# A second layer's set-up and edge scores placed in the wait for the first layer's expert rows, in a four-layer graph network on one core

## The chip, the cores and the metric

The kernel runs on one core of one Trainium2 chip. Its time is the device time of one execution in microseconds (us); the metric is the median over several executions. The core has five engines that run their own instruction streams side by side: TensorE (PE, matrix products), VectorE (DVE), ScalarE (ACT), GpSimd (POOL, which here issues the indirect gathers and scatters) and SyncE (SP, which here issues most of the plain DMAs). Each stream is in order: an instruction that waits holds back everything behind it on its engine.

## The reference, cut to what matters

The program takes `x` [3125, 256], 50,000 edges sorted by their target, and 32 attributes per edge. It runs four layers one after the other, and each layer is a graph part, a dense mixing part and a feed-forward part of experts, all added to `x`. What matters here is the feed-forward part of the first layer (L0), in which each token goes to one of 8 experts, and the graph part of the second layer (L1), a graph attention with 4 heads of 64:

```
# L0 feed-forward (top 1, capacity 489 tokens an expert)
x = x + prob * (relu(xe @ w1[e] + b1[e]) @ w2[e] + b2[e])     # xe: rows of layernorm(x)

# L1 graph part
x_proj = (xn @ lin_W.T).reshape(n, 4, 64)
s_src = einsum(x_proj, att_src); s_dst = einsum(x_proj, att_dst)
att = leaky(s_src[src] + s_dst[dst] + einsum((ea @ lin_edge_W.T), att_edge))
alpha = exp(att - segment_max(att, dst)); alpha = alpha / (sum over dst + 1e-12)
out = segment_sum(x_proj[src] * alpha, dst) + bias
```

The term with `ea` depends on the edges' attributes and on weights alone, not on `x`.

## The kernel before, in words

Tokens lie in 25 tiles of 128 rows, edges in 391 columns of 128. All of it is Python that writes one program; a scheduler then orders the instructions of each engine by the order in which they were written and by its own estimate of when each could start. Many lines are helpers: L145 is a matrix product, L153 and L155 are the copies out of PE's banks on ACT and DVE, L201 and L221 the layer norm, L425 and L419 the indirect scatter and gather.

**The first layer's experts.** `l0_ffn` (L1378) does the routing on DVE (softmax, first maximum, running counts: L331 to L1423), writes the 3,125 normed rows into the table `moe_buf` with 25 indirect scatters on POOL, and then goes through 8 experts. Of each it loads `w1`, `w2` (1 MB each) and `b2`, and the expert's rows `xb` (four loads, L1440); PE transposes them (L1445, into `xT`), multiplies by `w1` into `hT` and by `w2` into `y`. The `xb` loads wait for all 25 scatters. After the last expert, a check (`fin_ok`, L1474) decides a branch; in the branch taken, 25 gathers `yt` on POOL fetch the experts' rows, which are added to `x`, and the layer norm is worked out again.

**Work sent along.** Beside the experts run two other things. `route_scans` works out tables for a later layer on DVE and ACT. `Pump` issues the `cells` sends, 391 indirect scatters on POOL that fill a table of layer L2: 16 ahead of the experts, then one for every 700 columns that PE multiplies in `l0_ffn`, each bound to a product so that it doesn't run ahead, then 32 after the second layer's graph part, and the rest paced by products in `l1_ffn`, the second layer's experts. The pump is stopped after the last expert's products are written.

**The second layer's graph part.** After the branch, in this order of the program: `breaks` (L955) makes the masks `pen` and `penc`, which say where one target's edges end, out of 20 `dh` loads and one `dhc` load. `l1_near_setup` (L1551) loads weights, among them 12 small pieces of the attention vectors into `bd`, fills the table `l1seed` with a large negative number, makes 8 more columns of the weight `linw` and the 16-column weight `vedge`, and works out `sidx`, the place of each target's first edge. Then it goes through the 25 tiles (L1595 to L1604): a product `row` with the new columns, copies, a DMA that writes the row into the table `l1rows`, and a scatter of four numbers into `l1seed` (the seeds, L425, on POOL). It adds the bias to `x` (L1606), and `spread` (L983) reads the seeds back as `sh` and carries them to all edges by four scans into `pre`.

Then `drive` weaves four generators together. `gat_near` fetches the 391 columns of source rows with indirect gathers (L1072) into a `ring` of 44 places, adds `pre` to them (`att`), finds the maxima over each target, scales the rows, and sums them with PE (`seg`, L499); a ring place is free once its `seg` has run. `l1_mix_lean` is the dense mixing part, `norm_after` the norm that follows, and `l1_edge_scores` (L1610) works out the edges' own scores in 25 rounds: load 256 KB of `ea`, a product of 16 rows by 512 columns (L1619), a copy by ACT to `ez` (L1621), four small transposes (L1624), and an addition on DVE to `pre` (L1626). It has one `ez` buffer and two `ea` buffers.

Of the kernel before, what the change touches and what calls it, by code (L numbers as in the profile page):

```python
# [18 lines left out]
P = 128  # L19
# [100 lines left out]
class Net:  # L120
# [861 lines left out]

    def spread(self, pool, pre, seed, penc):  # L983

        nc = self.nc
        w = P + HALO
        per = penc.shape[0]
        sh = pool.tile([per, 4, w, 4], F32, name="sh")
        self.after_all(seed.name, nc.sync.dma_start(sh, self.lin(seed, 0, [[P * 4, per], [per * P * 4, 4], [1, w * 4]])))
        ps = [self.ps(4 * per) for _ in range(4)]  # L990
        for h in range(4):
            se = pool.tile([per, 4, w], F32, name="se")
            nc.vector.tensor_tensor_scan(se.rearrange("p q i -> p (q i)"), penc.rearrange("p q i -> p (q i)"),
                                         sh.rearrange("p q i h -> p (q i) h")[:, :, h], 0.0, OP.add, OP.max)
            for q in range(4):
                nc.tensor.transpose(ps[q][:, h * per:(h + 1) * per], se[:, q, HALO:], self.ident[:per, :per])
        for q in range(4):
            v = pre[:, q * per:(q + 1) * per, :]
            self.evac(v, ps[q].rearrange("p (h c) -> p c h", h=4))

# [376 lines left out]

    def l0_ffn(self, pool, lean=False, pr=None):  # L1378
        nc, a = self.nc, self.a
# [50 lines left out]
        mt = [(i * P, min(P, CAP - i * P)) for i in range(4)]  # L1430
        for e in range(NE):
            w1 = pool.tile([P, 2, FF], F32, name="w1", bufs=2)
# [3 lines left out]
            b2 = pool.tile([P, D], F32, name="b2", bufs=2)  # L1436
            nc.sync.dma_start(b2, bcast_rows(a["L0_ffn_b2"][e], D))
            xb = pool.tile([P, 4, D], F32, name="xb", bufs=2)
            for i, (m0, m) in enumerate(mt):
# [46 lines left out]
    def l0_combine(self, pool, ybuf, ri, prob):  # L1486

        nc = self.nc
        big = pool.tile([P, 2, D], F32, name="big")
        nc.vector.memset(big[:, 0, :], 1.0e4)  # L1490
        nc.vector.memset(big[:, 1, :], -1.0e4)
        top = 3.4028234663852886e38
        for t in range(T):
            y = self.gather(pool, "yt", ybuf, ri[:, t:t + 1], D, 4)
            nc.vector.tensor_scalar(y, y, prob[:, t:t + 1], None, op0=OP.mult)
            o = pool.tile([P, D], F32, name="yo", bufs=2)
            m = pool.tile([P, D], I32, name="ym", bufs=3)
            nc.vector.memset(o, 0.0)
            nc.vector.tensor_tensor(m, y, y, op=OP.is_equal)
            nc.vector.copy_predicated(o, m, y)  # L1500
            for j, (op, lim) in enumerate(((OP.is_gt, top), (OP.is_lt, -top))):
                m = pool.tile([P, D], I32, name="ym", bufs=3)
                nc.vector.tensor_scalar(m, o, lim, None, op0=op)
                nc.vector.copy_predicated(o, m, big[:, j, :])
            nc.vector.tensor_add(self.x[:, t, :], self.x[:, t, :], o)
# [44 lines left out]

    def l1_near_setup(self, keep, pool, pre, penc):  # L1551


# [13 lines left out]
        for k in range(2):  # L1567
            p = self.ps(8)
            self.mm(p, [(wn[:, o, k * P:(k + 1) * P], bd[:, o, :8]) for o in range(2)])
            nc.vector.tensor_copy(w[:, k, D:], p)  # L1570
        vb = keep.tile([P, 16], F32, name="vedge")
        nc.vector.memset(vb, 0.0)
# [8 lines left out]
        sidx = pool.tile([P, T], I32, name="sidx")  # L1581
        self.first_edges(sidx, self.deg)
        nrow = 393 * P
        seed = self.dram.tile([nrow, 4], F32, name="l1seed")
        neg = pool.tile([P, 262], F32, name="neg")
        nc.vector.memset(neg, -BIG)
        nc.sync.dma_start(self.lin(seed, 0, [[nrow * 4 // P, P], [262, 6], [1, 262]]),
                          neg[:, None, :].to_broadcast([P, 6, 262]))
# [3 lines left out]
        row = [pool.tile([P, 4, 66], F32, name=f"row{i}") for i in range(3)]  # L1592
        for r in row:
            nc.vector.memset(r[:, :, 64:65], 1.0)
        for t in range(T):  # L1595
# [14 lines left out]
    def l1_edge_scores(self, pool, pre, vb):  # L1610

        nc, a = self.nc, self.a
        pv = pre.rearrange("p (q j) h -> p j q h", q=4)
        for j0 in range(0, EG, 4):
            m = min(4, EG - j0)
            ea = pool.tile([P, 4 * P], F32, name="ea", bufs=2)
            nc.sync.dma_start(ea[:, :m * P], a["eaT"][:, j0 * P:(j0 + m) * P])
            p = self.ps(m * P, parts=16)
            nc.tensor.matmul(p, vb, ea[:, :m * P], start=True, stop=True)  # L1619
            ez = pool.tile([16, 4 * P], F32, name="ez")  # L1620
            nc.scalar.copy(ez[:, :m * P], p)  # L1621
            p = self.ps(16 * m)
            for j in range(m):
                nc.tensor.transpose(p[:, j * 16:(j + 1) * 16], ez[:, j * P:(j + 1) * P], self.ident[:16, :16])  # L1624
            v = pv[:, j0:j0 + m]
            nc.vector.tensor_add(v, v, p.rearrange("p (j q h) -> p j q h", q=4, h=4))  # L1626
            yield

# [925 lines left out]
    def route_scans(self, pool):  # L2554
# [3 lines left out]
        nc = self.nc  # L2558
        S, n = 4, C2
        lo = pool.tile([P, T2, n], BF16, name="r_lo")  # L2560
# [11 lines left out]
        for t in range(0, T2, S):  # L2572
            d = pool.tile([P, S, n], F32, name="r_d")
            wi = pool.tile([P, S, n], I32, name="r_wi")
            wl = pool.tile([P, S, n], I32, name="r_wl")
            out = pool.tile([P, 2, S, n], BF16, name="r_out")
# [504 lines left out]
    def fast(self):  # L3081
# [3 lines left out]
        with tc.tile_pool(name="keepf", bufs=1) as keep, tc.tile_pool(name="dramf", bufs=1, space=DRAM) as dram:  # L3085
# [30 lines left out]
            self.px = None  # L3116
            with Banks(self, **plain):
                send = self.send(cells, place, value[:, :, None], C1)
                for _ in range(16):
                    next(send)  # L3120
                with tp("ffn0") as p, tp("scan4") as sp:
                    self.pump = Pump(tc, send, 700)
                    beside(self.l0_ffn(p, True, pr0), (self.route_scans(sp), 1, 3))


            with tp("att1") as gp:
# [3 lines left out]
                nc.vector.tensor_scalar(nodeg, self.deg, 0.5, -BIG, op0=OP.is_lt, op1=OP.mult)  # L3130
                pen, penc = self.breaks(gp, self.dlin, C1)
                part, add_part = self.part_sums(keep)
                with Banks(self, **plain), tp("set1") as p:
                    table, aself, vb = self.l1_near_setup(gp, p, pre, penc)
# [5 lines left out]
                with Banks(self, mm=2, acc=1, ga=2, seg=2, px=1), tp("mix1") as mp:  # L3140
                    self.numbers()
                    self.one_hots = 2
                    close = self.gat_close(gp, table, 64, aself, nodeg, 1e-12, add_x)
                    drive((self.gat_near(gp, g, table, pre, pen, 64, close, RING, 12), 4), (self.l1_mix_lean(mp), 1),
                          (self.norm_after(closed, self.mixed, then=add_part), 1), (self.l1_edge_scores(mp, pre, vb), 2))
            self.px = None
# [365 lines left out]
```

## Time and profile before

The median of four executions is 3753.76 us (3748.79 to 3765.47). The profiled execution took 3758.31 us, with a span of 3756.2 us, so 2.1 us lie around the span. All times below are of the profiled execution.

| | us |
|---|---|
| PE busy in the span | 2946.5 (78%) |
| POOL busy | 2356.1 (63%) |
| DVE busy | 1885.0 (50%) |
| ACT busy | 890.6 (24%) |
| routing done (`wi`), first `moe_buf` scatter | 744.51, 744.98 |
| first `xb` load issued, first transpose of it | 778.48, 780.57 |
| last product of the last expert; `fin_ok`; first `yt` gather | 1017.81, 1020.00, 1031.86 |
| DVE goes on after the branch | 1077.42 |
| first seed scatter, first ring gather | 1114.48, 1146.95 |
| first `ea` load of the edge scores, first product | 1168.02, 1174.30 |

Busy time is the time in which an engine executes, summed over the span; the table's moments are us from the start of the span. Two instructions on different engines overlap, so busy times don't add up to the span. The granted clock (PEclk) is the share of full speed that TensorE was allowed.

### The profile page before, as it was taken

How to read it: one execution, taken by the hardware profiler on the slowest of the kernel's cores; microseconds unless marked ns; L12 is line 12 of the kernel's file. 1: busy time of each engine (PE TensorE's matmuls, PEld its weight loads, DVE VectorE, ACT ScalarE, POOL GpSimd, SP SyncE). 2: the span in 40 equal slices, each digit the busy share in tenths (PEclk: the TensorE clock that was granted, in tenths of full speed). 3: DMA queues.
4: the chain of work that ended last, by engine and by line, in shares of the span. 5: the costliest groups of instructions: out<-in, count | busy, mean ns of one | idle time of the engine just before them, and what ended most of it. 6: DMA issues, size and time to landing. Idle time of an engine off the chain costs nothing. (4 is left out here: it accounts for less than half of the span.)

```text
span 3756.2 us, 41484 instructions
## 1 busy us (share of the span) xinstructions
PE 2946.5 (78%) x12101; PEld 2093.4 (56%) x12101; DVE 1885.0 (50%) x5664; ACT 890.6 (24%) x1851; POOL 2356.1 (63%) x2316
## 2 busy tenths in 40 slices
PE   7576788569845766665998999369679899679999
PEld 3244565346532544543676888248556577457666
DVE  3176574431174966765991323531484711535665
ACT  2101001122111211111333211323222233334544
POOL 0368767667737777776775677467757664037771
PEclk9787787679956877877998999679889999789999
DMA  4897884433134434432224445158565523401110
GB/s 150 281 316 244 270 295 111 129 123 122 44 95 141 115 108 112 114 102 77 52 52 136 128 138 158 41 181 258 173 209 151 165 69 106 122 13 22 18 17 15
DMA packets 398304, 485.52 MB, mean 129 GB/s; under 512 B 100756, under 2 KB 317280, under 8 KB 397809
## 3 DMA queue, kind: packets, MB, share of 16 engines
q1 hardware_dynamic: 214128, 257.09, 22.8%
q0 software_dynamic: 88160, 129.89, 12.5%
q10 hardware_dynamic: 95776, 95.77, 7.6%
q8 instruction: 99, 1.62, 0.2%
q14 instruction: 141, 1.15, 0.1%
HBM read 324.71 MB, written 157.76 MB: 128 GB/s over the span
## 5 line engine op out<-in xcount | busy, mean ns | idle before, releaser
L540 POOL DMA_INDIRECT G<-h_tab,gi x391 | 415.8, 1064 | 282.3 <-DMA cl_w<-in_weight 119.9
L425 POOL DMA_INDIRECT cells<-count,turned x391 | 398.0, 1018 | 174.2 <-PE seg L905 60.3
L425 POOL DMA_INDIRECT cells<-value,place x391 | 421.0, 1077 | 132.9 <-PE mm L145 65.5
L905 PE MATMUL seg<-H,cells 128*128 128x256 f32 (+1 forms) x1875 | 478.9, 400 | 18.7 <-DMA cells<-cells 12.3
L1072 POOL DMA_INDIRECT ring<-l1rows,e1src x391 | 407.7, 1043 | 125.6 <-issue 74.0
L905 PEld LDWEIGHTS seg<-H,cells 128*128 128x128 f32 x1875 | 352.6, 191 | 101.4 <-DMA cells<-cells 20.9
L145 PE MATMUL mm<-w,hT 128*128 128x256 f32 (+1 forms) x1712 | 405.0, 388 | 0.0
L145 PE MATMUL mm<-xnT,w 128*128 128x512 f32 (+1 forms) x896 | 382.1, 568 | 6.4 <-DVE x L2876 5.9
L499 PE MATMUL seg<-G,E 128*128 128x257 f32 x782 | 270.5, 478 | 128.5 <-DMA G<-h_tab,gi 91.8
L425 POOL DMA_INDIRECT by_dst<-rec4i,place4i x256 | 263.2, 1028 | 161.7 <-issue 48.2
L145 PEld LDWEIGHTS mm<-w,hT 128*128 128x128 f32 (+1 forms) x1712 | 312.4, 190 | 55.7 <-issue 15.5
L499 PE MATMUL seg<-ring,E 128*128 128x264 f32 x782 | 255.9, 487 | 73.0 <-DVE E L493 72.7
L1072 POOL DMA_INDIRECT ring<-l3rows,e2src x256 | 243.7, 952 | 98.5 <-PE mm L145 32.6
L499 PEld LDWEIGHTS seg<-G,E 128*128 128x128 f32 x782 | 164.8, 231 | 219.7 <-DMA G<-h_tab,gi 108.9
L499 PEld LDWEIGHTS seg<-ring,E 128*128 128x128 f32 x782 | 181.3, 242 | 128.5 <-DVE E L493 84.2
L145 PEld LDWEIGHTS mm<-xnT,w 128*128 128x128 f32 x896 | 155.0, 194 | 133.3 <-issue 117.3
L201 PE MATMUL mm<-ident,xn 128*128 128x128 f32 x400 | 82.3, 360 | 161.0 <-DVE xn L221 116.9
L201 PEld LDWEIGHTS mm<-ident,xn 128*128 128x128 f32 x400 | 61.3, 183 | 181.9 <-DVE xn L221 70.0
L493 DVE TENSOR_TENSOR E<-px,e1dl 128x512 f32<-128x512 f32 x196 | 133.6, 682 | 31.9 <-PE seg L499 26.7
L1087 DVE TENSOR_TENSOR ring<-ring,px 128x1040 f32<-128x1040 f32 x98 | 120.3, 1227 | 1.1 <-ACT px L1063 1.0
L145 PE MATMUL mm<-xT,w 128*128 128x489 f32 x256 | 111.3, 593 | 7.3 <-DVE xT L155 7.3
L505 ACT COPY W_side<-seg 64x257 f32<-64x257 f32 (+2 forms) x126 | 40.9, 325 | 280.6 <-PE seg L499 272.1
(774 smaller groups left out, 5229.6 us busy)
## 6 DMA issues: line engine op xcount, KB each, us to landing
cells<-zeros ACTq DMA_DIRECT2D x80, 1024.0 KB
cells<-cells SPq DMA_DIRECT2D x250, 320.0 KB
ws<-in_L_ffn_expert_w SPq DMA_DIRECT2D x90, 256.0 KB
w<-in_L_ffn_w SPq DMA_DIRECT2D x16, 1024.0 KB
h_tab<-htab_s SPq DMA_DIRECT2D x25, 512.0 KB
r_b<-rowa SPq DMA_DIRECT2D x64, 128.0 KB
xb<-x_exp SPq DMA_DIRECT2D x30, 256.0 KB
y_exp<-ys ACTq DMA_DIRECT2D x30, 256.0 KB
```

Source lines behind the costliest of these rows:

```text
L145: m = self.nc.tensor.matmul(out, l, r, start=(i == 0), stop=(i == last))
L201: self.nc.tensor.transpose(p[:, i * P:(i + 1) * P], src(t0 + i)[:, k * P:(k + 1) * P], self.ident)
L425: return self.nc.gpsimd.indirect_dma_start(out=table, out_offset=bass.IndirectOffsetOnAxis(ap=idx, axis=0), in_=src, in_offset=None, bound ...
L493: nc.vector.tensor_tensor(A["hot"][:, :m], self.io(P)[:, None, :].to_broadcast([P, m, P]), g["dl"][:, c:c + m, None].to_broadcast([P, m, P ...
L499: self.product = nc.tensor.matmul(A["sum"], e, rows_c, start=(c == 0 or window(c - 1, nt) != k), stop=last).ins
L505: nc.scalar.copy(out, a[:, :w])
L540: nc.gpsimd.indirect_dma_start(out=ring[i % len(ring)][:, :wide], out_offset=None, in_=table, in_offset=bass.IndirectOffsetOnAxis(ap=gidx[ ...
L905: self.product = nc.tensor.matmul(acc, b[:, d * P:(d + 1) * P], h[:, i, :], start=(i == 0), stop=(i == T - 1)).ins
L1072: got = nc.gpsimd.indirect_dma_start(out=ring[:, i % size].rearrange("p h f -> p (h f)"), out_offset=None, in_=table, in_offset=bass.Indir ...
L1087: nc.vector.tensor_mul(v, v, EX[c // CB][:, c % CB:c % CB + m, :, None] .to_broadcast([P, m, 4, d + 1]))
```

## The change

1. `l1_near_setup` becomes a generator in three parts. The first runs ahead of `l0_ffn`: its loads, the `l1seed` fill and `sidx`. The second is handed to `l0_ffn` as `fill`, and is called after the 25 scatters and the first expert's weight loads are written: `vedge`, the 8 columns of `linw`, and all 25 rounds of `l1_edge_scores`. The third runs after the experts and writes table rows and seeds.
2. The edge scores use the room of the tile `hT` (four places for `ea`, three for `ez`); the transposes lag two rounds behind; the result is copied to `pre` and not added. They are no longer woven into `gat_near`. `spread` now adds to `pre`.
3. The masks (`breaks`) are made after the rows and ahead of `spread`.
4. In `l0_ffn`, the weights of the next expert are loaded ahead of the rows of this one, and the pump is stopped ahead of the last expert's products with `w2` (8,192 columns).
5. To make room, the branch that isn't taken (`l0_combine`) uses `hT`'s room too, and `route_scans` works on 2 columns at a time where it was 4, twice as often.

```diff
@@ spread
-            v = pre[:, q * per:(q + 1) * per, :]
-            self.evac(v, ps[q].rearrange("p (h c) -> p c h", h=4))
+            v, s = pre[:, q * per:(q + 1) * per, :], ps[q].rearrange("p (h c) -> p c h", h=4)
+            if add:
+                nc.vector.tensor_add(v, v, s)
+            else:
+                self.evac(v, s)
@@ l0_ffn
-        for e in range(NE):
+        W = {}
+
+        def weights(e):
             w1 = pool.tile([P, 2, FF], F32, name="w1", bufs=2)
...
+        weights(0)
+        if fill is not None:
+            fill(pool.tile([P, FF // P, CAP], F32, name="hT").rearrange("p f c -> p (f c)"))
+        for e in range(NE):
+            if e + 1 < NE:
+                weights(e + 1)
+            w1, w2, b2 = W.pop(e)
             xb = pool.tile([P, 4, D], F32, name="xb", bufs=2)
...
+            if e == NE - 1:
+                self.pump = None
             for i, (m0, m) in enumerate(mt):
@@ l1_near_setup (loads, seed table, neg, row, sidx now ahead of this)
+        room = yield
+        vb = pool.tile([P, 16], F32, name="vedge")
...
+        self.l1_edge_scores(room, pre, vb)
+        yield
         table = self.dram.tile([NP, D + 8], F32, name="l1rows")
...
-        self.spread(pool, pre, seed, penc)
-        return table, aself, vb
+        yield table, aself
+        with self.tc.tile_pool(name="sprd", bufs=1) as tmp:
+            self.spread(tmp, pre, seed, masks.pop(), add=True)
+        yield
@@ l1_edge_scores
+        def turn(j0, m, ez):
+            p = self.ps(16 * m)
+            for j in range(m):
+                nc.tensor.transpose(p[:, j * 16:(j + 1) * 16], ez[:, j * P:(j + 1) * P], self.ident[:16, :16])
+            nc.vector.tensor_copy(pv[:, j0:j0 + m], p.rearrange("p (j q h) -> p j q h", q=4, h=4))
+        for i, j0 in enumerate(range(0, EG, 4)):
+            m = min(4, EG - j0)
+            o = i % 4 * 512
+            ea = room[:, o:o + m * P]
+            nc.sync.dma_start(ea, a["eaT"][:, j0 * P:(j0 + m) * P])
+            p = self.ps(m * P, parts=16)
+            nc.tensor.matmul(p, vb, ea, start=True, stop=True)
+            o = 2048 + i % 3 * 512
+            ez = room[:16, o:o + m * P]
+            nc.scalar.copy(ez, p)
+            behind.append((j0, m, ez))
+            if len(behind) > 2:
+                turn(*behind.pop(0))
@@ the program
+                setup = self.l1_near_setup(gp, set1.__enter__(), pre, masks)
+                with Banks(self, **plain):
+                    next(setup)
...
+                        beside(self.l0_ffn(p, True, pr0, setup.send), (self.route_scans(sp), 2, 3))
+                    table, aself = next(setup)
+                set1.__exit__(None, None, None)
+                mask = tp("mask1")
+                pen, penc = self.breaks(mask.__enter__(), self.dlin, C1)
+                masks.append(penc)
+                with Banks(self, **plain):
+                    next(setup)
...
                     drive((self.gat_near(rp, g, table, pre, pen, 64, close, RING, 12), 4), (self.l1_mix_lean(mp), 1),
-                          (self.norm_after(closed, self.mixed, then=add_part), 1), (self.l1_edge_scores(mp, pre, vb), 2))
+                          (self.norm_after(closed, self.mixed, then=add_part), 1))
```

In the scheduled program of after, SP's stream holds the set-up's loads and the `l1seed` fill, the first expert's weights, 14 of the 25 `ea` loads (the second expert's weights among them), the first `xb` load, and then the other 11 `ea` loads between the `xb` loads of the first two experts. On PE all 25 rounds of the edge scores stand ahead of the first `xb` transposes. On DVE the `bd`, `neg` and `row` fills, the sums of `sidx` and four copies of `line` stand ahead of the routing's first softmax step. After the branch, two reductions of the mixing part (L1645) and the bias stand ahead of the first table row, and ten or so further operations of the mixing part lie between the rows; on SP 8 of the 20 `dh` loads stand ahead of the rows' DMAs, and the other mask loads and `sh` behind them.

More of the change, by code (lines that the diff above doesn't have):

```diff
@@ L981, in breaks, with spread @@
         return pen, penc
-    def spread(self, pool, pre, seed, penc):
+    def spread(self, pool, pre, seed, penc, add=False):
         nc = self.nc
@@ L1376, in l0_gate, with l0_ffn @@
         return pr, gate
-    def l0_ffn(self, pool, lean=False, pr=None):
+    def l0_ffn(self, pool, lean=False, pr=None, fill=None):
         nc, a = self.nc, self.a
@@ L1437, in l0_ffn @@
             nc.sync.dma_start(b2, bcast_rows(a["L0_ffn_b2"][e], D))
+            W[e] = w1, w2, b2
+        weights(0)
[5 more added lines that the diff above has]
+            w1, w2, b2 = W.pop(e)
             xb = pool.tile([P, 4, D], F32, name="xb", bufs=2)
@@ L1488, in l0_combine @@
         nc = self.nc
-        big = pool.tile([P, 2, D], F32, name="big")
-        nc.vector.memset(big[:, 0, :], 1.0e4)
-        nc.vector.memset(big[:, 1, :], -1.0e4)
+        room = pool.tile([P, 8, CAP], F32, name="hT").rearrange("p f c -> p (f c)")
+        part = lambda i: room[:, i * D:(i + 1) * D]
+        nc.vector.memset(part(0), 1.0e4)
+        nc.vector.memset(part(1), -1.0e4)
         top = 3.4028234663852886e38
@@ L1495, in l0_combine @@
             nc.vector.tensor_scalar(y, y, prob[:, t:t + 1], None, op0=OP.mult)
-            o = pool.tile([P, D], F32, name="yo", bufs=2)
-            m = pool.tile([P, D], I32, name="ym", bufs=3)
+            o = part(2 + t % 2)
+            m = part(4).bitcast(I32)
             nc.vector.memset(o, 0.0)
@@ L1501, in l0_combine @@
             for j, (op, lim) in enumerate(((OP.is_gt, top), (OP.is_lt, -top))):
-                m = pool.tile([P, D], I32, name="ym", bufs=3)
+                m = part(5 + j).bitcast(I32)
                 nc.vector.tensor_scalar(m, o, lim, None, op0=op)
-                nc.vector.copy_predicated(o, m, big[:, j, :])
+                nc.vector.copy_predicated(o, m, part(j))
             nc.vector.tensor_add(self.x[:, t, :], self.x[:, t, :], o)
@@ L1549, in l1_setup, with l1_near_setup @@
         return self.gat_tables("l1", pool, proj[:, :, :D], proj[:, :, D:D + 4], proj[:, :, D + 4:], 64)
-    def l1_near_setup(self, keep, pool, pre, penc):
+    def l1_near_setup(self, keep, pool, pre, masks):
         nc, a = self.nc, self.a
@@ L1566, in l1_near_setup @@
                                   bass.AP(tensor=s.tensor, offset=s.offset + h * 64, ap=[[1, 64], [1, 1]]))
[L1567 to L1571, printed above, removed]
+        nrow = 393 * P
+        seed = self.dram.tile([nrow, 4], F32, name="l1seed")
+        neg = pool.tile([P, 262], F32, name="neg")
+        nc.vector.memset(neg, -BIG)
+        nc.sync.dma_start(self.lin(seed, 0, [[nrow * 4 // P, P], [262, 6], [1, 262]]),
+                          neg[:, None, :].to_broadcast([P, 6, 262]))
+        row = [pool.tile([P, 4, 66], F32, name=f"row{i}") for i in range(3)]
+        for r in row:
+            nc.vector.memset(r[:, :, 64:65], 1.0)
+        sidx = pool.tile([P, T], I32, name="sidx")
+        self.first_edges(sidx, self.deg)
+        room = yield
+        vb = pool.tile([P, 16], F32, name="vedge")
         nc.vector.memset(vb, 0.0)
@@ L1579, in l1_near_setup @@
             nc.vector.tensor_copy(vb[q * 32:(q + 1) * 32, q * 4:q * 4 + 4], p[q * 32:(q + 1) * 32, :])
[L1581 to L1588, printed above, removed]
+        for k in range(2):
+            p = self.ps(8)
+            self.mm(p, [(wn[:, o, k * P:(k + 1) * P], bd[:, o, :8]) for o in range(2)])
+            nc.vector.tensor_copy(w[:, k, D:], p)
+        self.l1_edge_scores(room, pre, vb)
+        yield
         table = self.dram.tile([NP, D + 8], F32, name="l1rows")
@@ L1591, in l1_near_setup @@
         aself = keep.tile([P, T, 4], F32, name="aself")
-        row = [pool.tile([P, 4, 66], F32, name=f"row{i}") for i in range(3)]
-        for r in row:
-            nc.vector.memset(r[:, :, 64:65], 1.0)
         for t in range(T):
@@ L1606, in l1_near_setup, with l1_edge_scores @@
         nc.vector.tensor_add(self.x, self.x, bias[:, None, :].to_broadcast([P, T, D]))
-        self.spread(pool, pre, seed, penc)
-        return table, aself, vb
-    def l1_edge_scores(self, pool, pre, vb):
+        yield table, aself
+        with self.tc.tile_pool(name="sprd", bufs=1) as tmp:
+            self.spread(tmp, pre, seed, masks.pop(), add=True)
+        yield
+    def l1_edge_scores(self, room, pre, vb):
         nc, a = self.nc, self.a
         pv = pre.rearrange("p (q j) h -> p j q h", q=4)
[L1614 to L1621, printed above, removed]
+        behind = []
+        def turn(j0, m, ez):
             p = self.ps(16 * m)
@@ L1624, in l1_edge_scores @@
                 nc.tensor.transpose(p[:, j * 16:(j + 1) * 16], ez[:, j * P:(j + 1) * P], self.ident[:16, :16])
-            v = pv[:, j0:j0 + m]
-            nc.vector.tensor_add(v, v, p.rearrange("p (j q h) -> p j q h", q=4, h=4))
-            yield
+            nc.vector.tensor_copy(pv[:, j0:j0 + m], p.rearrange("p (j q h) -> p j q h", q=4, h=4))
[12 more added lines that the diff above has]
+                turn(*behind.pop(0))
+        for b in behind:
+            turn(*b)
     def l1_mix_lean(self, pool):
@@ L2558, in route_scans @@
         nc = self.nc
-        S, n = 4, C2
+        S, n = 2, C2
         lo = pool.tile([P, T2, n], BF16, name="r_lo")
@@ L2574, in route_scans @@
             wi = pool.tile([P, S, n], I32, name="r_wi")
-            wl = pool.tile([P, S, n], I32, name="r_wl")
+            wl = d.bitcast(I32)
             out = pool.tile([P, 2, S, n], BF16, name="r_out")
@@ L3116, in fast @@
             self.px = None
[L3117 to L3123, printed above, removed]
             with tp("att1") as gp:
@@ L3130, in fast @@
                 nc.vector.tensor_scalar(nodeg, self.deg, 0.5, -BIG, op0=OP.is_lt, op1=OP.mult)
-                pen, penc = self.breaks(gp, self.dlin, C1)
                 part, add_part = self.part_sums(keep)
-                with Banks(self, **plain), tp("set1") as p:
-                    table, aself, vb = self.l1_near_setup(gp, p, pre, penc)
+                masks = []
+                set1 = tp("set1")
+                setup = self.l1_near_setup(gp, set1.__enter__(), pre, masks)
+                with Banks(self, **plain):
+                    next(setup)
+                    send = self.send(cells, place, value[:, :, None], C1)
+                    for _ in range(16):
+                        next(send)
+                    with tp("ffn0") as p, tp("scan4") as sp:
+                        self.pump = Pump(tc, send, 700)
+                        beside(self.l0_ffn(p, True, pr0, setup.send), (self.route_scans(sp), 2, 3))
[6 more added lines that the diff above has]
+                    next(setup)
                 def add_x(t, o):
@@ L3139, in add_x @@
                     closed.add(t)
-                with Banks(self, mm=2, acc=1, ga=2, seg=2, px=1), tp("mix1") as mp:
+                with Banks(self, mm=2, acc=1, ga=2, seg=2, px=1), tp("ring1") as rp, tp("mix1") as mp:
                     self.numbers()
                     self.one_hots = 2
-                    close = self.gat_close(gp, table, 64, aself, nodeg, 1e-12, add_x)
-                    drive((self.gat_near(gp, g, table, pre, pen, 64, close, RING, 12), 4), (self.l1_mix_lean(mp), 1),
-                          (self.norm_after(closed, self.mixed, then=add_part), 1), (self.l1_edge_scores(mp, pre, vb), 2))
+                    close = self.gat_close(rp, table, 64, aself, nodeg, 1e-12, add_x)
+                    drive((self.gat_near(rp, g, table, pre, pen, 64, close, RING, 12), 4), (self.l1_mix_lean(mp), 1),
+                          (self.norm_after(closed, self.mixed, then=add_part), 1))
+                mask.__exit__(None, None, None)
             self.px = None
```

## The prediction

> **What bounds the kernel now.** I read the busy time by stretch first, then the order of time around three places where an engine stands still, then the costliest groups. In the stretches the columns are PE, PE's weight loads, DVE, ACT, POOL (busy us and instructions), granted PE clock, DMA share, GB/s.
>
> ```profile
> 745.00:780.00 35.00, 0.00 (x0) 0.00 (x0) 0.20 (x1) 0.00 (x0) 24.58 (x25) 0.50 0.27 97
> 790.00:1018.00 228.00, 221.25 (x819) 148.09 (x817) 56.51 (x170) 52.53 (x76) 175.84 (x171) 0.99 0.32 99
> 1077.00:1105.00 28.00, 3.58 (x16) 3.48 (x16) 19.01 (x30) 0.00 (x0) 0.00 (x0) 0.50 0.26 69
> 1105.00:1147.00 42.00, 24.48 (x102) 20.35 (x102) 17.72 (x123) 4.49 (x12) 24.66 (x26) 0.78 0.33 104
> 1147.00:1215.00 68.00, 39.02 (x128) 15.35 (x129) 34.40 (x51) 12.78 (x21) 50.11 (x44) 0.58 0.59 169
> 1215.00:1680.00 465.00, 317.36 (x1209) 231.09 (x1208) 339.93 (x796) 73.14 (x158) 357.56 (x347) 0.79 0.41 113
> ```
>
> To be seen: 35 us in which only POOL works (the `moe_buf` scatters); then a stage that PE fills (221 of 228); then 70 us of set-up, 28 of them without POOL; then a stage paced by POOL, 391 ring gathers, each 0.95 busy and 0.30 of issue.
>
> The wait before the experts, as SP and PE show it, and SP's list of waits (total, times, longest):
>
> ```profile
> 778.48 3.63 SPq L1440 DMA_DIRECT2D xb<-moe_buf  x8
> 780.57 2.37 PE L1445 MATMUL mm<-ident,xb 128*128 128x128 f32 x8 [39.15 <-DMA xb<-moe_buf]
> SPq L1440 <- DMA moe_buf<-xn,wi: 43.4, 3, 40.9
> ```
>
> SP itself stands 40.9 us at the first `xb` load. Whatever is queued behind that load stands too.
>
> After the experts, sends that POOL still owes hold back the gathers that end the layer:
>
> ```profile
> 1020.00 0.16 DVE L1474 TENSOR_SCALAR fin_ok<-mm 128x1 int32<-128x1 f32 x1 [0.47 <-PE mm L1473]
> 1030.57 0.98 POOL L425 DMA_INDIRECT cells<-value,place  x1 [0.30 <-issue]
> 1031.86 0.99 POOL L419 DMA_INDIRECT yt<-moe_y,ri  x1 [0.30 <-issue]
> ```
>
> And the set-up with the ring's start: first seed, first gather, the two full-ring waits, and rounds of the edge scores at the slow and at the full clock:
>
> ```profile
> 1114.48 1.02 POOL L425 DMA_INDIRECT l1seed<-sd,sidx  x1 [47.69 <-DVE row L1600]
> 1146.95 0.99 POOL L1072 DMA_INDIRECT ring<-l1rows,e1src  x1 [0.30 <-issue]
> 1215.47 0.94 POOL L1072 DMA_INDIRECT ring<-l1rows,e1src  x1 [5.26 <-PE seg L499]
> 1243.35 0.95 POOL L1072 DMA_INDIRECT ring<-l1rows,e1src  x1 [1.88 <-PE seg L499]
> ...
> 1177.42 1.89 PE L1619 MATMUL mm<-ea,vedge 128*16 128x512 f32 x2
> 1180.03 0.60 PE L1624 MATMUL mm<-ident,ez 16*128 16x16 f32 x4 [0.72 <-ACT ez L1621]
> 1180.56 1.89 PE L1619 MATMUL mm<-ea,vedge 128*16 128x512 f32 x2
> 1204.83 1.03 PE L1619 MATMUL mm<-ea,vedge 128*16 128x512 f32 x2
> 1206.88 0.42 PE L1624 MATMUL mm<-ident,ez 16*128 16x16 f32 x4
> ```
>
> **Part 1: the fill, a cost.** All 25 edge rounds stand ahead of the first `xb` transpose on PE, so their end sets when the experts start.
> - Routing: between the last gate value (735.13) and the first softmax step DVE now also has the sums of `sidx` (some 26 operations of 0.16 to 0.19, as they ran at 1106 to 1113) and 4 copies of `line` (0.50 in all), about 5.5 us, and inside the chain 6 small copies (0.15 to 0.2), 1 us. So the scatters start 6.5 later, near 751.5, end near 784, and `xb` can be issued at 785.
> - SP: the set-up's DMAs took 10.6 us there (1093.30 to 1103.86); from 726.7 on, with 2 us of weights, they are done near 740, in a wait that lasts to 785. They cost nothing; without that cover, 10.6. Fourteen `ea` loads follow, and their rounds at 2.4 to 3.1 us end by 785.
> - The other 11 `ea` loads are behind the first `xb` load, whose wait ends at 785. The load-to-PE time at `xb` was 2.1 us, so round 15 starts at 787. A round takes 1.82+0.53 = 2.35 us at the slow clock and 0.96+0.35 = 1.31 at the full one, start to start. The rounds from 1174 to 1196 stayed slow with PE idle 0.72 of every 3.14 us; full clock came after the dense stretch from 1198 to 1203, and the first expert's weight loads too went from 0.82 to 0.41 us apart within 4.5 us. With the lag of two rounds PE no longer waits for `ez`, and four places for `ea` cover the load. I take 4 us slow (1.7 rounds) and 9.3 rounds at 1.31: done near 803, 1 us more for the last transposes: 804, against 780.6, or 23.5 late. The first expert's own slow start (4.5 us at half speed) is then gone, 2.5 back. **Cost 21.** If all 11 stay slow, done at 814 to 816 and nothing back: 34. Low end: 16, if `ea` flows at once at full clock.
> - The Trainium skill (TensorE: Matmul & The Clock Gate, Part 1: The HAM clock gate) says that the array goes from half to full speed after one busy window of some 3.4 us, however few or many products. The rows at 1174 to 1196 show 22 us at 77% busy without that. By the rule the cost is 21, by the row 34.
>
> The experts stay PE-bound, so the lateness goes through to 1020. `route_scans` has the same elements in twice as many instructions, with DVE at 56.51 and ACT at 52.53 of 228: covered.
>
> **Part 2: sends, a gain and a debt.** 8,192 columns at 700 a send are 12 sends. Ten were owed after `fin_ok` (1020.27 to 1031.5). The last expert's products with `w2` take PE some 14 us, enough for the backlog, so `yt` starts 1 to 3 us after `fin_ok` and not 11.9: **10 back** (9 to 11). The 12 go to `l1_ffn`, where POOL ran its sends almost back to back to 1987.76; they add 12 x 1.29 = 15.5, to 2004.2. The loads of the filled cells were issued at 2001.87, and PE waited for them (first `seg` of layer L2 at 2008.57). With 2 us from the last send to the load, that is 2006: **4 lost** (0 to 6).
>
> **Part 3: set-up after the branch, a gain.** T is the moment at which DVE goes on (1077.42 before); the first ring gather came at T+69.5. Now nothing ahead of the rows waits for masks or small loads. DVE has two reductions (1.48 each, as at 1166.78) and the bias (6.83): first row copy at T+10. The 25 rows need 0.75 of DVE each, 19 us, and ten operations of `l1_mix_lean` that now lie between them 16 us: last row near T+45. Seeds (25 x 1.29) run behind the rows from T+11, and the last ends near T+48; ring gathers from T+49 or T+50. **20 back** (13 to 24; the low end if seeds beside these 1.5 us operations lengthen, as the gathers beside such ones did: 2.26 at 1161.06 beside a scan of 1.56).
>
> Behind the rows come masks and `sh`. SP has 8 of the 20 `dh` loads ahead of the rows' DMAs (8 x 0.65, by T+7, under the bias) and 12 behind them (7.8); the masks took 16 us of DVE with their waits for loads (1077.59 to 1093.65), some 10 busy: masks done near T+61, `sh` in at T+66, scans and copies as before (11 us) to T+77, first `att` T+81. Before, `att` to first `seg` was 1193.63 to 1214.5, 21 us: T+102. The ring is full 44 x 1.26 = 55.5 after its first gather, T+105. So the masks' 16 us are covered, by 3 us only; each us beyond costs one.
>
> **Part 4: the ring stage.** The edge rounds leave it: 33.1 us of products and 11.8 of transposes on PE, 25 small additions on DVE. POOL sets its pace, so only the two full-ring waits (7.2) and some of the lengthened gathers can come back; ones near masks may lengthen. **6 back** (-6 to +15).
>
> **Sum.** -21 + 10 - 4 + 20 + 6 = 11 us. Against the profiled 3758.3 that is 3747; the profiled execution lies 4.55 above the median, so 3742.5 by the median. A measurement of this kernel can tell some 0.3%, 11.3 us, from no change; the sum stands on that edge.
>
> **Rivals.**
> - *Slower: the fill ends late.* The one mechanism is the in-order wait of SP at `xb`: rounds 15 to 25 only begin at 787. It speaks for it that PE's clock before the experts was 0.50 and slow rounds lasted 22 us; against, that nothing now breaks the rounds. Price: 34 if they stay slow, 40 if loads also come in singly behind `xb`; I take 37. With the low ends 13 from the set-up and -2 from the ring, and 10 - 4: -37 + 13 + 6 - 2 = -20, 3774. It decides from a fill cost of 32 on (21 + 11). Chance 0.22.
> - *No gain kept: the ring fills before the masks are there.* If `pre` comes 10 to 15 us later than T+77, POOL stands as long at its 45th gather, and the sum goes to -4 to +1: 3753 to 3758. For: cover of 3 us. Against: 8 of the masks' loads now land long before. Chance 0.18.
> - *Larger gain.* Fill 16, set-up 24, ring 12: 26, 3728. For: lengthened gathers in the ring's first stretch lay beside scans and mixing operations, half of which move ahead of it. Chance 0.20.
> - *Full hiding,* were no `ea` load held: fill 4, sum 28, 3726; the order on SP speaks against it, 0.03.
> - *Forecast as summed,* 3735 to 3750: 0.37.
>
> The bound for faster is 3742.5. Three fifths of the forecast (0.22) and both larger gains (0.23) lie under it: faster 0.45. The rest of the forecast (0.15) and most of the case with no gain kept (0.14 of 0.18) lie within: 0.29. The late fill and what is left are slower: 0.26. The range takes in the larger gain and the late fill: 3716 to 3778.
>
> **What would show it.** Right: first `xb` transposes at 802 to 806, with a granted clock near 1 from about 792; SP's `ea` loads split by the wait at `xb`; first `yt` within 3 us of `fin_ok`; first ring gather 48 to 52 us after DVE goes on; no wait over 2 us at the 45th gather. Wrong: first transposes after 812 (slow rounds) or before 795 (not held), a ring wait over 5 us, or cells of L2 loaded more than 6 us later against the second layer's end.

## The result

The changed kernel takes 3761.59 us (median of 45 executions, 3751.3 to 3771.84) against 3753.7 for the kernel before (74 executions). The ratio is 1.0020, with a 95% interval of 1.0014 to 1.0026: slower by 0.2%, some 7.5 us. The forecast was 0.3% faster (3742.5), and its sign is wrong. The profiled execution took 3759.15 us, with a span of 3757.4.

The same views as in the prediction, now of the changed kernel. First the stretches (PE, PE's weight loads, DVE, ACT, POOL, granted clock, DMA share, GB/s): scatters and fill, experts, rows with seeds, the time after the seeds, ring.

```profile
738.00:791.00 53.00, 40.34 (x146) 11.76 (x147) 5.52 (x26) 14.14 (x25) 24.61 (x25) 0.74 0.72 247
791.00:1028.00 237.00, 227.81 (x842) 151.73 (x840) 63.52 (x198) 55.64 (x87) 171.66 (x171) 0.99 0.31 96
1085.00:1122.00 37.00, 20.26 (x76) 15.43 (x76) 25.54 (x101) 5.40 (x13) 29.30 (x25) 0.78 0.36 110
1122.00:1156.00 34.00, 3.63 (x16) 2.46 (x16) 16.54 (x21) 0.00 (x0) 0.00 (x0) 0.50 0.21 63
1156.00:1672.00 516.00, 325.13 (x1170) 247.22 (x1170) 347.73 (x800) 67.04 (x147) 396.66 (x391) 0.74 0.40 109
```

The fourth line is the surprise: 34 us in which POOL does nothing, between the last seed and the first ring gather. In the order of time, of the changed kernel:

```profile
771.83 0.33 SPq L1453 DMA_DIRECT2D xb<-moe_buf  x1
791.22 1.06 PE L1458 MATMUL mm<-ident,xb 128*128 128x128 f32 x8
1027.47 0.16 DVE L1489 TENSOR_SCALAR fin_ok<-mm 128x1 int32<-128x1 f32 x1 [0.47 <-PE mm L1488]
1029.30 0.99 POOL L419 DMA_INDIRECT yt<-moe_y,ri  x1 [7.83 <-issue]
1120.80 0.98 POOL L425 DMA_INDIRECT l1seed<-sd,sidx  x1 [0.31 <-issue]
1123.40 1.28 DVE L973 TENSOR_TENSOR pen<-dh 64x1035 bf16<-64x1035 f32 x1 [10.20 <-DMA l1seed<-sd,sidx]
1145.12 1.56 DVE L993 TENSOR_TENSOR_SCAN se<-penc,sh 98x672 f32<-98x672 bf16 x1 [5.77 <-DMA sh<-l1seed]
1153.13 1.56 DVE L993 TENSOR_TENSOR_SCAN se<-penc,sh 98x672 f32<-98x672 bf16 x1 [1.01 <-PE mm L996]
1154.75 0.92 PE L996 MATMUL mm<-ident,se 98*128 98x98 f32 x4 [1.65 <-DVE se L993]
1155.21 1.98 DVE L1000 TENSOR_TENSOR pre<-pre,mm 128x392 f32<-128x392 f32 x4 [0.52 <-PE mm L996]
1156.54 0.99 POOL L1075 DMA_INDIRECT ring<-l1rows,e1src  x1 [34.76 <-DVE pre L1000]
```

The experts start right where the fill ends (no idle time before 791.22), and `yt` follows `fin_ok` by 1.8 us, as forecast. But the first mask operation waits 10.2 us for the seeds' scatters, which it does not read, and the first ring gather waits 34.76 us for the chain of masks and spread, of which it reads nothing either. The profile puts this wait down to the first addition to `pre` (L1000), the last event before the gather; taken one by one, POOL's waits end with DVE's last scan (L993, done at 1154.7) and PE's last transposes of its result `se` (L996, done at 1155.7). The only tie is memory. The set-up's pool is given back ahead of the masks' pool, and the pool of the spread ahead of the ring's, so that `pen` lies where the seeds' source lay, and the ring where `dh`, `dhc`, `sh` and `se` lay. Of the loads, the wait list of the first ring gather in the changed program names the last `dh`, `dhc` and `sh`; that of the kernel before names the row DMAs alone.

Stage by stage, in us. "Again" is a second profile of the kernel before (the experiment before_again). DVE's going on after the branch is called T, as in the prediction.

| stage | before | again | changed | ring_apart | no_edge | sidx_late_2 | fill_first_2 | near_edges |
|---|---|---|---|---|---|---|---|---|
| last `G` gather to first scatter | 35.4 | 35.7 | 38.3 | 38.2 | 39.1 | 36.5 | 36.9 | 36.5 |
| first scatter to first `xb` transpose | 35.6 | 35.7 | 52.9 | 52.7 | 35.7 | 55.0 | 49.4 | 35.8 |
| to `fin_ok` | 239.4 | 239.8 | 236.2 | 235.9 | 239.0 | 235.9 | 237.0 | 240.0 |
| to first `yt` | 11.9 | 10.6 | 1.8 | 1.8 | 1.8 | 1.8 | 1.8 | 1.8 |
| to T | 45.6 | 45.5 | 45.5 | 45.6 | 45.7 | 45.8 | 45.5 | 46.0 |
| T to first ring gather | 69.5 | 70.7 | 81.7 | 49.7 | 82.4 | 50.4 | 50.5 | 53.3 |
| first to last ring gather | 532.1 | 533.9 | 514.9 | 518.7 | 519.5 | 517.0 | 518.8 | 522.3 |
| to the first gather of `l1_ffn` | 59.1 | 58.7 | 57.9 | 57.6 | 57.2 | 56.5 | 57.5 | 57.4 |
| to the first `seg` of layer L2 | 270.4 | 269.9 | 273.0 | 269.8 | 270.1 | 270.4 | 269.5 | 268.0 |
| from there to the end of the span | 1747.7 | 1755.2 | 1755.1 | 1758.1 | 1758.3 | 1758.6 | 1756.2 | 1759.3 |

Against the first profile of before, the stages down to layer L2 add up to +3.2 us, against the second to +1.7. Where the rest of the 7.5 lies, one profile of each kernel cannot show: the two profiles of before are themselves 7.5 apart in the last stage.

### The profile page after: what moved, and what is told of

Same layout as the page of the kernel before. It is cut to its first block, busy times and chain, and to the rows that moved or that the text cites. A ratio compares the mean times of both kernels' runs of the same rounds, so it can differ in the third digit from the quotient of the medians.

```text
span 3757.4 us, 41520 instructions
## 1 busy us (share of the span) xinstructions
PE 2960.9 (79%) x12101; PEld 2107.0 (56%) x12101; DVE 1888.6 (50%) x5686; ACT 887.0 (24%) x1855; POOL 2340.1 (62%) x2316
## 5 line engine op out<-in xcount | busy, mean ns | idle before, releaser
L1075 POOL DMA_INDIRECT ring<-l1rows,e1src x391 | 397.0, 1015 | 153.6 <-issue 75.6
L1090 DVE TENSOR_TENSOR ring<-ring,px 128x1040 f32<-128x1040 f32 x98 | 120.1, 1226 | 0.5 <-ACT px L1066 0.2
L1039 PE MATMUL ga<-ident,att 128*64 128x40 f32 (+1 forms) x246 | 33.0, 285 | 97.6 <-DVE att L1035 93.7
```

Of the source, the lines that this page charges most:

```text
L1039: nc.tensor.matmul(p[:, o:o + w], att[:, c0 + k:c0 + k + CB, :].rearrange("p c h -> p (c h)"), self.ident[:, i:i + w], start=True, stop=True)
L1075: got = nc.gpsimd.indirect_dma_start(out=ring[:, i % size].rearrange("p h f -> p (h f)"), out_offset=None, in_=table, in_offset=bass.Indir ...
L1090: nc.vector.tensor_mul(v, v, EX[c // CB][:, c % CB:c % CB + m, :, None] .to_broadcast([P, m, 4, d + 1]))
```

## The experiments

Theory A: the time went into waits that the reuse of memory makes, ahead of the masks and above all ahead of the ring. Theory B: it went into the later start of the experts, and the ring stage is bound by the masks' chain in any case. Where not said otherwise, a kernel is an edit of the changed kernel, and ratios are to the kernel before on the same chip.

**ring_apart.** The ring's tile comes from a pool of its own, opened ahead of the masks.

```diff
                 set1.__exit__(None, None, None)
+                rooms = tp("hold1")
+                ring1 = rooms.__enter__().tile([P, RING, 4, 66], F32, name="ring")
                 mask = tp("mask1")
...
-                    drive((self.gat_near(rp, g, table, pre, pen, 64, close, RING, 12), 4), (self.l1_mix_lean(mp), 1),
+                    drive((self.gat_near(rp, g, table, pre, pen, 64, close, RING, 12, ring1), 4), (self.l1_mix_lean(mp), 1),
```

> The changed kernel with one difference: the ring's tile is taken from a pool of its own, opened after the set-up's memory is given back and ahead of the masks. Theory A (memory): the ring of the changed kernel lies where the masks' loads and the seeds' copy lay, so its first gather waits for them (34.8 us in the profile), and the masks in turn lie where the seeds' source lay, so that they wait for the last seed (10.2 us). Then the first ring gather comes 47 to 51 us after DVE goes on, not 81.7, the masks lie among rows and seeds, and the kernel is 25 us faster than the changed one (17 to 34): 3728 to 3745, below the kernel before. Theory B (the fill): what was lost is the later start of the experts, and the ring stage is bound by the masks' chain anyway; then gathers start earlier but POOL stands at the 45th gather, and the time stays within 5 us of 3761.

3731.71 us, ratio 0.9927 (0.9909 to 0.9945): 30 us under the changed kernel by the medians, 35 by the two ratios. The order of time in ring_apart:

```profile
1093.94 1.23 DVE L973 TENSOR_TENSOR pen<-dh 64x1035 bf16<-64x1035 f32 x1
1122.84 1.48 POOL L425 DMA_INDIRECT l1seed<-sd,sidx  x1 [0.30 <-issue]
1127.24 2.30 POOL L1076 DMA_INDIRECT ring<-l1rows,e1src  x1 [2.92 <-DMA sh<-l1seed]
1141.99 1.98 DVE L1000 TENSOR_TENSOR pre<-pre,mm 128x392 f32<-128x392 f32 x4 [0.52 <-PE mm L996]
1155.76 0.28 DVE L1033 TENSOR_TENSOR att<-ring,pre 128x68 f32<-128x68 f32 x1 [9.91 <-DMA ring<-l1rows,e1src]
1164.82 10.32 PE L499 MATMUL seg<-ring,E 128*128 128x264 f32 x32 [4.03 <-DVE E L493]
```

Not a line of the computation differs, and the first gather comes 15 us ahead of the additions to `pre` and not in their midst. As the ring's tile now covers the set-up's old place, the masks lie above it and run among the rows (1093.94), with seeds still to come. The gather still waits 2.92 us; the profile names `sh`, but what POOL's waits held for was the landing of the last seeds (1125.5), whose source lay at that place. The first `att` waits 9.91 us for gathered rows, so the masks are not what it waits for, and the first `seg` is there 37.6 us after the first gather, before the ring is full. Theory A holds, theory B's second half falls; its first half, the later start of the experts, is measured next.

**no_edge.** The 25 edge rounds are left out.

```diff
-        self.l1_edge_scores(room, pre, vb)
+        nc.vector.memset(pre, 0.0)
```

> The changed kernel with the 25 rounds of the edges' own scores left out (the tile they fill is set to zero instead; the output then lacks that term). It measures what the fill costs where it stands. By the traces the first xb transposes come 52.9 us after the first moe_buf scatter with the rounds and came 35.6 after it in the kernel before: 17 us less, minus 2.5 for the experts' slow start that comes back: 14 less than the changed kernel, 3747 (3742 to 3752). If the fill costs nothing, within 3 us of 3761. The wait of the ring for the seeds' copy stays (some 82 us after DVE goes on) by theory A.

3747.85 us, ratio 0.9973 (0.9960 to 0.9986): 13.7 less than the changed kernel by the medians, some 18 by the two ratios. The table has it where it was expected: 17.2 less to the first transpose, 2.8 more in the experts. So the rounds cost 14 us where they stand, and without them the 82.4 us to the ring stay.

**ea_act.** The `ea` loads are issued by ACT's queue.

```diff
-            nc.sync.dma_start(ea, a["eaT"][:, j0 * P:(j0 + m) * P])
+            nc.scalar.dma_start(ea, a["eaT"][:, j0 * P:(j0 + m) * P])
```

> The changed kernel with the 25 ea loads issued from ACT's queue, so that none stands behind the wait for the scatters on SP. Theory A (memory): the ring's start relative to DVE's going on stays at 82 us; only the fill gets shorter, with the first xb transposes 38 to 44 us after the first moe_buf scatter where it was 52.9, and the time is 9 to 15 us less than the changed kernel's: 3747 to 3752. Theory B (the fill is what cost): the same. Rival C: the loads are bound by bandwidth behind 4 MB of weights, not by the queue; then the transposes stay at 50 to 53 and the time within 3 us of the changed kernel's.

3766.82 us, ratio 1.0023 (1.0010 to 1.0037), the same as the changed kernel; the transposes come 52.0 us after the first scatter. It took the hold away in small part only: 18 `ea` loads, not 14, were issued ahead of the first `xb` load. ACT in ea_act:

```profile
779.35 0.35 ACTq L1644 DMA_DIRECT2D hT<-in_eaT  x1
779.80 0.57 ACT L1649 COPY hT<-mm 16x512 f32<-16x512 f32 x1 [6.32 <-DMA xb<-moe_buf]
```

ACT stood until the `xb` loads had gone, though they are on another queue: in the program's wait lists the loads of all queues count on the same eight semaphores (counters that a load raises once it has landed), and a load waits for the earlier one on its semaphore. The transposes lie where rival C put them, but as seven loads were held all the same, that does not show its mechanism. The test says that changing the queue is no help, not that the hold costs nothing.

**ring_ea.** Both edits.

> Both edits: the ring in memory of its own, and the ea loads on ACT's queue. If the two waits are independent (theory A with the fill's held loads) the gains add: 25 + 11, some 3725 (3715 to 3738). If the ring stage is bound by the masks' chain (theory B) it is as with ACT's queue alone, 3747 to 3752.

3733.03 us, ratio 0.9937 (0.9919 to 0.9954): inside the range expected, but as ring_apart alone. The gains did not add, since ea_act had none.

**sidx_late and fill_first.** Both start from ring_apart. The first moves the sums of `sidx` into the fill; the second also writes the fill ahead of the first weights.

```diff
-        self.first_edges(sidx, self.deg)
         room = yield
+        self.first_edges(sidx, self.deg)
... fill_first, in l0_ffn:
-        weights(0)
         if fill is not None:
             fill(pool.tile([P, FF // P, CAP], F32, name="hT").rearrange("p f c -> p (f c)"))
+        weights(0)
```

> ring_apart with the sums of sidx moved from ahead of the routing to behind it (into the fill). The prediction's first term says that they hold the softmax back by 5.5 us: then the first moe_buf scatter comes 32 to 34 us after the last G gather (38.2 in ring_apart), the first xb transposes likewise, and the time is 3 to 6 us less than ring_apart's 3731.7. Rival: the edge rounds, not the scatters, set the start of the experts; then the scatters are earlier, the transposes come as much later after them, and the time stays within 2 us.

> As sidx_late, and the fill is written ahead of the first expert's weight loads, so that 24 of the 25 ea loads stand ahead of the first xb load on SP. If the held loads and the weights ahead of them are what makes the fill late, the first xb transposes come 36 to 44 us after the first scatter (52.7 in ring_apart) and the time is 10 to 18 us under ring_apart's: 3714 to 3722. Rival: the weights now come late themselves or the ea loads are as slow at the head of the queue (bandwidth shared with the scatters); then the transposes or the products with w1 wait, and the gain is under 5 us.

They first ran on a chip where the kernel before itself takes 4322.8 us: ratios 0.9993 (0.9966 to 1.0020) and 1.0018 (0.9998 to 1.0038) there, so no gain at all. Their profiles say where it went. The ring starts 51.1 and 51.9 us after T, much as on the other chips; the two profiles of pump_only (below), whose set-up is that of the kernel before, have 74.9 and 74.5 here. But the first transposes come 120.6 and 121.5 us after the last `G` gather, against 86.3 and 84.1 in pump_only: with the fill the experts start some 35 us later here, 15 to 20 on the other chips. Why was not tested. Both ran again where the kernel before takes 3761 us:

> sidx_late again, beside kernels that it is to be compared with, since it ran on a chip on which the kernel before took 4323 us. Expected as for sidx_late: first scatter 32 to 34 us after the last G gather (38.2), 3 to 6 us under ring_apart's 3731.7 if the scatters set the start of the experts; within 2 us of it if the edge rounds do.

> fill_first again, for the same reason. If held loads and the weights ahead of them make the fill late, first xb transposes 36 to 44 us after the first scatter (52.7) and 10 to 18 us under ring_apart (3714 to 3722); if bandwidth or the rounds themselves set it, under 5 us of gain.

sidx_late_2 took 3728.91 us, ratio 0.9920 (0.9900 to 0.9940), which can't be told from ring_apart. The scatters come 1.7 us earlier after the last `G` gather (36.5, not the 32 to 34 expected), and the transposes 2.3 later after the scatters: the edge rounds, not the scatters, set the start of the experts. fill_first_2 took 3723.96 us, 0.9912 (0.9893 to 0.9931). The transposes come 49.4 us after the first scatter where 36 to 44 were expected. In fill_first_2 all but one `ea` load stand ahead of `xb`, yet:

```profile
742.15 0.44 SPq L1441 DMA_DIRECT2D w<-in_L_ffn_w  x1
743.10 4.95 SPq L1645 DMA_DIRECT2D hT<-in_eaT  x4
753.26 1.87 PE L1647 MATMUL mm<-hT,vedge 128*16 128x512 f32 x2 [5.22 <-DMA hT<-in_eaT]
768.31 1.87 PE L1647 MATMUL mm<-hT,vedge 128*16 128x512 f32 x2 [2.11 <-DMA hT<-in_eaT]
779.47 0.33 SPq L1454 DMA_DIRECT2D xb<-moe_buf  x1
```

PE still waits for `ea` loads (5.22 and 2.11 us) and runs at the slow clock after each of these waits, and the first `xb` load itself is now issued at 779.47, behind the `ea` loads, 43.2 us after the first scatter where it was 33.5. The edit did not put the weights behind the fill, either: in SP's order those of two experts still stand among the `ea` loads. The load that PE waits for at 753.26 was issued at 743.10, right behind a 1 MB weight load (742.15), and landed 10.0 us later by its semaphore. The gain over ring_apart is 7.7 us by the medians, between the two forecasts, and the intervals overlap.

**near_edges.** sidx_late with the fill undone: the rounds go back among the ring's gathers.

```diff
-        self.l1_edge_scores(room, pre, vb)
         yield
...
-                          (self.norm_after(closed, self.mixed, then=add_part), 1))
+                          (self.norm_after(closed, self.mixed, then=add_part), 1), (self.l1_edge_scores(mp, pre, vb), 2))
```

> sidx_late with the edge rounds put back among the ring's gathers, as in the kernel before (one ez, two ea, an addition to pre); set-up, masks and ring stay as in sidx_late. It undoes the fill alone. The experts then start as before, 35.6 us after the first scatter, which gives 15 us against sidx_late; the ring stage gets the rounds back, 532 us long as before where it was 515 to 519, or longer, since the first gathers now come earlier than pre: 13 to 25 us. By the prediction's sums the fill costs about as much as it gives: within 8 us of sidx_late. If the fill was the mistake of the change, 10 us or more faster than sidx_late; if it is worth its 14 us, 10 us or more slower.

3726.73 us, ratio 0.9911 (0.9894 to 0.9929), against sidx_late_2's 3728.91: no difference that the intervals could tell. The experts start 19.2 us earlier after the first scatter and take 4.1 longer with their slow start, so that the rounds cost 15.1 in the fill. Back among the gathers they cost 5.3 in the ring, where 13 to 25 were expected. The stage before it is 2.9 longer too, but no round runs in it (the first product is at 1136.29, the first gather at 1118.66): the seeds took 2.8 us longer, some of them beside operations of the mixing part, and that the rounds' return caused this is not shown. By its stages the fill is worth nothing, and may lose 7 to 10 us; by the medians nothing can be told.

**before_again.**

> The kernel before, unchanged, for a second profile. If the 10 us by which the changed kernel's first graph stage was shorter (567 us from first to last G gather, 578 before), and the 7.5 us by which everything after the second layer was longer, belong to single executions, this profile lies near 567 and 1755 there. If they belong to the change, it shows 578 and 1748 again.

3759.96 us in its one execution. The first graph stage is 569 us from first to last `G` gather and the last stage 1755.2, both as in the changed kernel: those two differences belong to executions, and the term-by-term accounts below use the stages between.

**pump_only.** The kernel before with the pump's stop alone (`if lean and e == NE - 1: self.pump = None`, ahead of the products with `w2`).

> The kernel before with one part of the change: the pump is stopped ahead of the last expert's products with w2. Expected by the prediction's second part: the first yt gather 1 to 3 us after fin_ok (11.9 before), and 4 us (0 to 6) lost at the second layer's end; 6 us faster than before (3748). Rival: the 12 sends come back in full behind the second layer's experts (15.5 - 10): no gain or 5 us slower. Its stages ahead of the experts are those of before, so that it also shows whether the first graph stage (577.9 us from first to last G gather in the profile of before, 563 to 569 in the others) differs by the change or by the execution.

> pump_only again (the kernel before, with the pump stopped ahead of the last expert's products with w2), since it ran on a chip on which the kernel before took 4323 us. By the stages of the changed kernel: first yt gather 1.8 us after fin_ok (10.6 and 11.9 before) and 0 to 3 us more from the second layer's weight gathers to the first seg of layer L2 (270): 7 to 10 us less than before, 3744 to 3747, ratio 0.997 to 0.998. Rival: the 12 sends come back in full later: the ratio holds 1.

Both times it ran where the kernel before takes 4323 us, with the ratio 1.0015 (0.9996 to 1.0034): no gain there. Its experts last 286.5 us there and not 239.4, with PE waiting 29.4 us for `xT`; sends paced by slower products probably owe nothing at the end, but the kernel before was not profiled on that chip. What the stop is worth on the others is read from stages alone: 8.8 to 10.1 us to the first `yt`, and between -2 and +3 us ahead of layer L2. Its net time was not measured there.

## Why the prediction was wrong

**Part 3 is the step that failed.** "Ring gathers from T+49 or T+50" took POOL to be free once the last seed was issued, and asked only when the ring would be full. The last seed was issued at T+46, near the forecast, though not for the reason given: the last row was done at T+38 and not T+45, and the seeds took 29.3 us of POOL and not the 24.6 of before, as six of them lengthened. What was missing is that the ring's tile had moved: from the pool `att1`, opened ahead of the masks and the set-up, into "ring1", opened after the masks' loads and the spread had given their memory back. The ring gather thus waited for the end of the very chain that the prediction had running beside it: 81.7 us after T, where ring_apart, with the ring elsewhere, has 49.7. These 32 us are more than the whole forecast gain. That ring_apart meets the forecast of T+49 or T+50 is in part luck: its seeds end at T+46.8, a little early, and a wait of 2.92 us by memory, which the prediction did not have, fills the rest. The rival with the ring full before the masks are there had the right place, but the wrong mechanism and under half of the price (10 to 15).

**The masks' cover failed for the same reason.** The prediction had them end at T+61; they began at T+48.6, after 10.2 us of waiting for the seeds, where they were to start behind the last row at T+45, and `pre` was done at T+82 where T+77 was forecast. The ring never filled up, since it started after all of it.

**Part 1 was near.** The first transposes came 20.2 us later after the last `G` gather (against the first profile of before), and 3.2 came back in the experts: 17.0 against 21 forecast. Of its terms, the routing was over-sized (2.9, not 6.5: DVE had already waited 4.70 us for the iota at 731.77, and the sums of `sidx` filled that). The eleven held rounds took 15.2 us from 775.25 to 790.42, 16 forecast. The held rounds were at the full clock by 779.09, 3.8 us after they began, and 4 were forecast. The Trainium skill (TensorE: Matmul & The Clock Gate, Part 1: The HAM clock gate) has some 3.4 us for this, and the trace agrees. The row at 77% busy, with an idle 0.72 us in each round, did not bear on rounds that follow without a gap.

**Part 2 held.** 11.9 to 1.8 us, 10 back as forecast (though nine sends, not ten, stood between `fin_ok` and the first `yt` before). The debt was 2.6 in the changed kernel (4 forecast) and not to be seen in ring_apart.

**Part 4 was too small.** The ring stage took 17.2 us less, 6 forecast: the two full-ring waits (7.1) are gone, and gathers are 10.7 us shorter in all (407.7 busy before, 397.0 after). Some 4 of it come with the late start, when the spread no longer lies beside gathers: with the ring started early the stage is 13.4 shorter.

The sum by what was measured, against the first profile of before: the start of the experts 17.0 lost, sends 10.1 gained, debt 2.6 lost, set-up 12.2 lost (20 gained in the forecast), 0.1 gained up to T, ring 17.2 and the stage behind it 1.2 gained: 3.2 lost. With the ring apart the same stages add up to 28.9 saved down to layer L2, and the kernel is 0.7% faster than before, though not on the chip of 4323 us, where the two kernels built on it gained nothing.

On the other chips the best versions are ring_apart and those built on it; fill_first_2, at 3723.96 us, beats both kernels by 0.9% or more (1.0020 and 0.9912).

## What to carry to other kernels

When a change moves a tile to another pool, look up what lay at that place before and who reads it last: the new owner's first instruction waits for that, whatever its data say, and a prefetch that is meant to run beside a chain must not lie where the chain's buffers lay. The wait list of the first instruction of each moved stage shows it before anything has run; the order of instructions alone does not. And work that is moved into an idle stretch is worth only what it held up at its old place: here 25 rounds cost 15 us in the new place and 5 to 8 in the old.

## What the runs showed of the hardware

- Loads took longer to land behind large loads. In the changed kernel the first `ea` load (256 KB) was issued at 730.46, 2.6 us after the first of two 1 MB weight loads, and PE's first product waited for it until 740.59: 10.1 us. By their semaphores, `ea` loads issued at 779.19 and 780.50 landed after 2.8.
- In the changed kernel a ring gather of 0.95 us lengthened to as much as 3.48 beside the mixing part's 128x1280 operations with two inputs in on-chip memory (L1675, L1683, L1687, L1689). Of 40 meetings with one of them 31 were those of a gather of over 1.2 us. Of 148 meetings with L1090, which also has two inputs, one of them (`px`) in PE's banks, 5 were.

```profile
1184.11 0.47 DVE L1047 TENSOR_TENSOR_SCAN bw<-pen,ga 64x168 f32<-64x168 bf16 x1
1184.50 1.46 DVE L1689 TENSOR_TENSOR kv<-kv,rb_L_mix_vln_bias 128x1280 f32<-128x1280 f32 x1
1184.91 3.48 POOL L1075 DMA_INDIRECT ring<-l1rows,e1src  x1 [0.31 <-issue]
1186.08 1.48 DVE L1675 TENSOR_TENSOR xh<-xn,hm 128x1280 f32<-128x1280 f32 x1
```

- One chip ran the same program 15% slower (4323 against 3754 us), at the same length of most single instructions, with gaps on PE that wait for nothing the profile shows (287 us in all in fill_first there, 5 in fill_first_2 on another chip):

```profile
847.77 1.89 PE L1647 MATMUL mm<-hT,vedge 128*16 128x512 f32 x2 [5.56 <-issue]
859.73 1.89 PE L1647 MATMUL mm<-hT,vedge 128*16 128x512 f32 x2 [6.75 <-issue]
```

What makes these gaps was not tested.
